# Writing a sampling table in larger pieces, with the image blocks kept in SBUF and two late writes

## The chip, the core and the metric

The kernel runs on one core of one Trainium2 chip. The metric is the device time of one execution in microseconds, the median of three runs. Profiles are taken in an execution of their own, in which every instruction is recorded; that one ran longer (8957 us) than the timed ones (7859 us). Times of single instructions below are from that profile.

## The reference

Four layers run one after the other on an input of 4 images, 256 channels, 64 x 64 pixels, all in float32. Each layer normalises its input (group norm, 32 groups), applies a block and adds the input. Only the first block matters here, a deformable convolution:

```
y    = leaky_relu(bn(conv1x1(gn(x))))                       # 256 -> 256
xp   = y @ inproj_w.T + inproj_b                            # values to be sampled
t    = leaky_relu(bn(depthwise3x3(y)))
offset, mask = t @ off_w.T + off_b, softmax(t @ mask_w.T + mask_b)
samp = bilinear sample of the padded xp, 4 groups of 64 channels,
       9 points a pixel and group, at place + 6 * tap + offset
dout = sum over the 9 points of samp * mask, then outproj
x2   = bn(y + dout); squeeze-and-excite; fc1, leaky_relu, fc2; result y + mlp
```

The three others are a linear attention block with depthwise 5x5 convolutions, a 3x3 convolution with binarised weights, and an attention block over pooled keys.

## The kernel before

An image is held as 128 partitions (channels) by two halves of channels (`KT` = 2) by 4096 pixels, and worked on in eight blocks of 512 pixels, which is eight rows of 64.

**Sampling.** For each image n the values xp lie in device memory in a table `tab[n]` of shape [4 groups, 66, 67, 2, 64]: at a place (y, x) it has the 64 channels of a group for this row (s = 0) and for the row below (s = 1). So 1024 bytes in a row are all four neighbours that a bilinear sample needs, and every value stands in the table twice. `sample(n)` goes over the points in rounds of 14 pixels. A round issues four gathers on GpSimd (L592, 128 places each, one a group), TensorE sums them with the weights that VectorE made (`wm`, L583), and later steps transpose, project and add. There are 1172 gathers an image. The gathered data have seven buffers of four.

**What makes the table.** `convolve(n)` first loads the image's eight blocks for the statistics (L334), computes the group norm, and writes zeros to the table's edges (L347 to L353, 48 small writes). Then `steps()` (L405) goes over the blocks again, in half blocks of 128 output channels: it loads x once more (L409; tag `x`, four buffers); `convolved` makes the 1x1 convolution in PSUM (L367), whose leaky relu gives `yc` (L369 on ScalarE, L370 on VectorE); `spread` copies it into the padded tiles of the depthwise convolution and writes the block to `y_d[n]` (L376); `projected` multiplies `yc` by `inproj_w` with pixels on the output's partitions (L387): 128 pixels at a time, thus two rows of the image; `added` adds the bias into `xo` (L391) and makes x + y + bias in place in x (L393), which goes to `xy_d[n]` (L396) for the end of the layer. Last come 16 writes of a block's `xo` to the table (L401), of 256 pieces of 256 bytes each:

```
for r in range(2):          # which of the two rows of a tile of 128 pixels
    for s in range(2):      # as this row, or as the row below
        for j in range(4):  # which tile
```

`offsets` works on chunks of two blocks: depthwise 3x3 (L185, L187), offsets and mask (L486 to L489), coordinates and weights (`coordinates`), which go to `s_d[n]` (L542). `sample` reads them back as `sl` (L572, L573).

**Order of the work.** `run` interleaves generators by shares of their cost (`beside`). In the start-up `convolve(0)` and the first chunk of `offsets` run alone, and every engine's order is made by the framework's scheduler from priorities (the order of the program text) and its cost model. Afterwards sections with `ordered()` keep the order of the program text on TensorE, VectorE, ScalarE and GpSimd; the DMA queue of SyncE (SP) is ordered by the scheduler throughout, and executes in that order. Five such sections matter: `sample(0)` beside `convolve(1)` to `convolve(3)` and the remaining offsets; `sample(1)` beside the binarising of weights, the feed-forward and linear attention of image 0; `sample(2)` and `sample(3)` beside the later layers of the images before; and then a tail without sampling.

Of the kernel before, what the change touches and what calls it, by code (L numbers as in the profile page):

```python
# [9 lines left out]
F32 = mybir.dt.float32  # L10
I32 = mybir.dt.int32
AF = mybir.ActivationFunctionType
ALU = mybir.AluOpType
# [4 lines left out]
P = 128  # L18
N, C, H, W = 4, 256, 64, 64
HW = H * W  # L20
KT = C // P
NB = HW // 512
NT = HW // P
G, PT = 4, 9
# [46 lines left out]

class Net:
    def __init__(self, ctx, tc, a, out):
        self.tc, self.nc, self.a, self.out = tc, tc.nc, a, out
        e = ctx.enter_context
        self.cp = e(tc.tile_pool(name="const", bufs=1, side="left"))
        self.ps1 = e(tc.tile_pool(name="ps1", bufs=1, space=PSUM))
        self.mm = e(tc.tile_pool(name="mm", bufs=3, space=PSUM))
        self.banks, self.alone = cycle(["mm"]), False
        self.dp = e(tc.tile_pool(name="scratch", bufs=1, space=DRAM))  # L80
# [246 lines left out]
    def convolve(self, n, w, sp, bp, pads, used):  # L327


        nc, a = self.nc, self.a  # L330
        src = a["x"][n].rearrange("(k p) s -> p k s", p=P)
        st = sp.tile([P, KT, NB, 6], F32, name="st")
        for b in range(NB):
            self.stats(st, self.block(bp, src, b, "x", bufs=4), b)  # L334
            yield 1.5
        sc, bi = yield from self.groupnorm(sp, st, "g0")
        cw = sp.tile([P, KT, C], F32, name="cwf")
        sh = self.folded(sp, cw, w["cw"], sc, bi, "g0")
        nc.vector.tensor_tensor(sh, sh, self.sh[:, 0:KT], ALU.add)
        low = sp.tile([P, KT], F32, name="low")  # L340
        nc.vector.tensor_scalar(low, sh, SLOPE, None, ALU.mult)
        yield 4


        tab, z = self.tab[n], self.zero
        for g in range(G):
            nc.sync.dma_start(tab[g, 0, :, 0, :], z[0:TX, 0:64])  # L347
            nc.sync.dma_start(tab[g, TY - 2, :, 1, :], z[0:TX, 0:64])
            nc.sync.dma_start(tab[g, TY - 1].rearrange("x s c -> x (s c)"), z[0:TX, 0:P])
            for xx in (0, TX - 2, TX - 1):  # L350
                nc.sync.dma_start(tab[g, 1:TY - 2, xx].rearrange("y s c -> y (s c)"), z[0:TY - 3, 0:P])
                nc.sync.dma_start(tab[g, 0, xx:xx + 1, 1, :], z[0:1, 0:64])
                nc.sync.dma_start(tab[g, TY - 2, xx:xx + 1, 0, :], z[0:1, 0:64])  # L353
        yield 2

        new = lambda c: self.padded(bp, KT, 18, 1, c, bufs=3)
        rw = lambda v: v.rearrange("p (r w) -> p r w", w=W)

        later, now = {}, 0

        def after(lag, f, *args):
            later.setdefault(now + lag, []).append(partial(f, *args))

        def convolved(b, x, yb, m):
            ps = self.ps1.tile([P, 512], F32, name="cv", tag="vk")
            for k in range(KT):
                nc.tensor.matmul(ps, cw[:, k, m * P:(m + 1) * P], x[:, k], start=k == 0, stop=k == KT - 1)  # L367
            t = bp.tile([P, 512], F32, name="lk")
            after(1, lambda: nc.scalar.activation(t, ps, AF.Identity, bias=low[:, m:m + 1], scale=SLOPE))  # L369
            after(1, lambda: nc.vector.scalar_tensor_tensor(yb[:, m], ps, sh[:, m:m + 1], t, ALU.add, ALU.max))  # L370
            after(2, spread, b, yb, m)

        def spread(b, yb, m):
            self.spread({c: p[:, m] for c, p in own.items()}, rw(yb[:, m]), b, 1)
            if m:
                nc.sync.dma_start(self.y_d[n][:, :, b * 512:(b + 1) * 512], yb)  # L376
                c, h = divmod(b, 2)
                for ready in [c - 1] * (b > 0 and not h) + [c] * (b == NB - 1):
                    pads.append((n, ready, own.pop(ready)))

        def projected(b, x, yb, xo, j2):

            ps = self.ps().rearrange("p (j o) -> p j o", o=C)
            for j in range(2):
                at = (2 * j2 + j) * P
                for k in range(KT):
                    nc.tensor.matmul(ps[:, j], yb[:, k, at:at + P], w["iw"][:, k], start=k == 0, stop=k == KT - 1)  # L387
            after(1, added, b, x, yb, xo, j2, ps)

        def added(b, x, yb, xo, j2, ps):  # L390
            nc.vector.tensor_tensor(xo[:, 2 * j2:2 * j2 + 2, :], ps,  # L391
                                    self.row("inproj_b").unsqueeze(1).to_broadcast([P, 2, C]), ALU.add)
            nc.vector.scalar_tensor_tensor(x[:, j2], yb[:, j2], self.vec("fc2_b", j2), x[:, j2], ALU.add, ALU.add)  # L393
            if not j2:
                return
            nc.sync.dma_start(self.xy_d[n][:, :, b * 512:(b + 1) * 512], x)  # L396
            for r in range(2):
                for s in range(2):
                    for j in range(4):
                        yi = 8 * b + 2 * j + r + 1 - s  # L400
                        nc.sync.dma_start(  # L401
                            tab[:, yi, 1:W + 1, s, :].rearrange("g x c -> x g c"),
                            xo[r * 64:(r + 1) * 64, j, :].rearrange("p (g c) -> p g c", g=G))

        def steps():  # L405
            last = None
            for b in range(NB + 1):
                if b < NB:
                    x = self.block(bp, src, b, "x", bufs=4)  # L409
                    yb = bp.tile([P, KT, 512], F32, name="yc", bufs=3)  # L410
                for m in range(KT):
                    if b < NB:
                        if not m and (not b or b % 2 and b // 2 + 1 < NCH):
                            need[now + 1] = (b + 1) // 2
                        convolved(b, x, yb, m)
                    yield 2
                    if last:
                        if not m:
                            xo = bp.tile([P, 4, C], F32, name="xo")
                        projected(*last, xo, m)  # L420
                    yield 2
                last = b, x, yb

        own, need = {}, {}
        for cost in steps():
            yield cost
            now += 1
            if now in need:
                while len(own) + len(pads) - len(used) > 2:
                    yield 0  # L430
                own[need[now]] = new(need[now])
            for f in later.pop(now, ()):
                f()
# [869 lines left out]
```

## Time and profile before

| What | Value |
|---|---|
| Time, median of 3 | 7858.98 us (7857.48 to 7888.82) |
| Span of the profiled execution | 8957.1 us |
| Busy share PE, DVE, ACT, POOL | 67%, 58%, 24%, 58% |
| First gather of images 0, 1, 2, 3 at | 189.8, 1983.3, 3751.3, 5591.8 us |
| Last gather of image 3 at | 7429.4 us |
| DMA moved | 1059 MB, 819976 packets, 464320 of them under 512 bytes |
| Table writes (L401) | 512, 64 KB each |
| Loads of the input x | 64, 512 KB each |

PE is the matrix engine (PEld its loading of weights), DVE the vector engine, ACT the scalar engine, POOL GpSimd, SP the engine that issues DMAs. A group of instructions is shown by line, engine, operation, and what it writes and reads; then the busy time in us, the mean of one in ns, and the idle time of the engine in front of it, with what ended most of that. A float32 matrix product appears in the records as two passes.

### The profile page before, as it was taken

How to read it: one execution, taken by the hardware profiler on the slowest of the kernel's cores; microseconds unless marked ns; L12 is line 12 of the kernel's file. 1: busy time of each engine (PE TensorE's matmuls, PEld its weight loads, DVE VectorE, ACT ScalarE, POOL GpSimd, SP SyncE). 2: the span in 40 equal slices, each digit the busy share in tenths (PEclk: the TensorE clock that was granted, in tenths of full speed). 3: DMA queues.
4: the chain of work that ended last, by engine and by line, in shares of the span. 5: the costliest groups of instructions: out<-in, count | busy, mean ns of one | idle time of the engine just before them, and what ended most of it. 6: DMA issues, size and time to landing. Idle time of an engine off the chain costs nothing. (4 is left out here: it accounts for less than half of the span.)

```text
span 8957.1 us, 94935 instructions
## 1 busy us (share of the span) xinstructions
PE 6029.8 (67%) x36020; PEld 3636.8 (41%) x36020; DVE 5176.0 (58%) x6393; ACT 2190.6 (24%) x4899; POOL 5162.6 (58%) x4950
## 2 busy tenths in 40 slices
PE   3354554447744447688776677887766778987899
PEld 2232332223422223244554443345544433664477
DVE  4344443443366667524777776227777772599734
ACT  1111111112211111122223222222232222455424
POOL 1666666566666666666666656666666561376410
PEclk7566675668866667799987787898878889998899
DMA  6455454445533334444443334444544333220131
GB/s 166 119 152 158 135 160 130 131 125 161 161 105 104 104 106 124 122 133 135 133 138 110 110 112 135 139 136 128 142 116 115 108 116 97 71 71 27 45 96 55
DMA packets 819976, 1059.01 MB, mean 118 GB/s; under 512 B 464320, under 2 KB 524864, under 8 KB 817984
## 3 DMA queue, kind: packets, MB, share of 16 engines
q0 software_dynamic: 225024, 614.77, 23.9%
q1 hardware_dynamic: 594496, 438.18, 17.1%
q8 instruction: 285, 4.67, 0.2%
q14 instruction: 171, 1.40, 0.0%
HBM read 883.86 MB, written 168.69 MB: 118 GB/s over the span
## 5 line engine op out<-in xcount | busy, mean ns | idle before, releaser
L592 POOL DMA_INDIRECT g<-tab,sl x4688 | 4628.4, 987 | 2800.6 <-issue 1224.9
L185 DVE SCALAR_TENSOR_TENSOR agg<-pad,vec,agg 128x1024 f32<-128x1024 f32 x2280 | 2934.3, 1287 | 61.7
L599 PE MATMUL acc<-g,wm 128*32 128x128 f32 x18752 | 1027.0, 336 | 2144.7 <-ACT at L604 1593.1
L599 PEld LDWEIGHTS acc<-g,wm 128*32 128x32 f32 x18752 | 564.6, 129 | 2620.9 <-ACT at L604 1791.9
L583 DVE TENSOR_TENSOR wm<-con,sl 128x1024 f32<-128x1024 f32 (+1 forms) x296 | 358.2, 1211 | 720.7 <-remote 575.2
L1018 PE MATMUL ps<-xd,w 128*128 128x256 f32 x3072 | 746.0, 395 | 31.5 <-issue 23.6
L624 ACT COPY dT<-dp 64x112 f32<-64x112 f32 x1176 | 286.9, 244 | 1543.1 <-remote 734.7
L1018 PEld LDWEIGHTS ps<-xd,w 128*128 128x128 f32 x3072 | 594.8, 199 | 150.7 <-issue 66.9
L717 PE MATMUL ps<-x2f,f 128*128 128x512 f32 x1024 | 503.1, 642 | 7.1 <-ACT f L708 4.0
L788 PE MATMUL ps<-xr,qw 128*128 128x512 f32 x768 | 474.4, 750 | 21.4 <-issue 8.2
L174 DVE SCALAR_TENSOR_TENSOR hm<-ps,vec,lk 128x512 f32<-128x512 f32 x256 | 190.7, 750 | 497.5 <-ACT lk L173 394.4
L724 PE MATMUL ps<-hm,f 128*128 128x512 f32 x1024 | 457.7, 601 | 0.1
L604 ACT COPY at<-acc 128x256 f32<-128x256 f32 (+1 forms) x588 | 218.5, 372 | 731.3 <-remote 670.3
L969 POOL TENSOR_TENSOR xd<-xp 128x640 f32<-128x640 f32 x64 | 79.5, 1270 | 507.0 <-ACT xp L981 412.7
L632 PE MATMUL po<-dT,ow 128*128 128x224 f32 (+1 forms) x1216 | 318.2, 414 | 51.5 <-DVE hm L174 15.6
L836 ACT COPY kt<-pt 128x512 f32<-128x512 f32 x256 | 149.7, 585 | 792.1 <-remote 350.7
L173 ACT ACTIVATE lk<-ps,low 128x512 f32<-128x512 f32 x256 | 174.1, 687 | 625.2 <-PE ps L717 479.1
L1128 PEld LDWEIGHTS ps<-gt,pT 128*128 128x128 f32 x2048 | 288.9, 222 | 70.7 <-issue 40.4
L1128 PE MATMUL ps<-gt,pT 128*128 128x128 f32 x2048 | 302.1, 309 | 17.3 <-ACT pT L1124 11.7
L201 POOL TENSOR_TENSOR ak<-ak,m 128x1024 f32<-128x1024 f32 x96 | 227.9, 2373 | 147.1 <-ACT m L200 143.6
L1108 PE MATMUL s<-ph,th 128*128 128x512 f32 x512 | 289.3, 674 | 26.8 <-ACT kt L836 10.0
L632 PEld LDWEIGHTS po<-dT,ow 128*128 128x128 f32 x1216 | 263.3, 231 | 105.7 <-issue 46.4
(243 smaller groups left out, 8071.3 us busy)
## 6 DMA issues: line engine op xcount, KB each, us to landing
g<-tab,sl POOLq DMA_INDIRECT x4688
x<-x SPq DMA_DIRECT2D x128, 512.0 KB
xr<-x SPq DMA_DIRECT2D x96, 512.0 KB
x<-in_x SPq DMA_DIRECT2D x64, 512.0 KB
tab<-xo SPq DMA_DIRECT2D x512, 64.0 KB
y<-yc SPq DMA_DIRECT2D x32, 512.0 KB
x2f<-x SPq DMA_DIRECT2D x32, 512.0 KB
xyf<-x SPq DMA_DIRECT2D x32, 512.0 KB
```

Source lines behind the costliest of these rows:

```text
L185: nc.vector.scalar_tensor_tensor(to, s, wt, acc, ALU.mult, ALU.add)
L583: nc.vector.tensor_tensor(wm[:, 0:nu], self.con("own").unsqueeze(1).unsqueeze(1).to_broadcast(sh), sl[:, r:r + nu, G:].unsqueeze(3).to_bro ...
L592: nc.gpsimd.indirect_dma_start(out=g[:, i, :], out_offset=None, in_=table, in_offset=bass.IndirectOffsetOnAxis(ap=sl.bitcast(I32)[:, r, i: ...
L599: nc.tensor.matmul(acc[32 * i:32 * i + 32, :], wm[:, r4, 4 * i + 2 * x:4 * i + 2 * x + 2, :], g[:, i, x * P:(x + 1) * P], start=x == 0, st ...
L624: nc.scalar.copy(dT[b][hs, :, q0:q0 + m * (v1 - v0)].rearrange("p g (v o) -> p g v o", o=m), dp[u][hs, v0:v1, :, s, 0:m].rearrange("p v g ...
L632: nc.tensor.matmul(po[m][:, 0:np_], self.ow[:, k, m * P:(m + 1) * P], dT[b][:, k, 0:np_], start=k == 0, stop=k == G - 1)
L717: nc.tensor.matmul(ps, f1[:, k, m * P:(m + 1) * P], x2[:, k], start=k == 0, stop=k == KT - 1)
L724: nc.tensor.matmul(ps, f2[:, k, m * P:(m + 1) * P], hm[:, k], start=k == 0, stop=k == 4 * KT - 1)
L788: nc.tensor.matmul(ps, qw[:, k, m * P:(m + 1) * P], x[:, k], start=k == 0, stop=k == KT - 1)
L1018: nc.tensor.matmul(ps[:, e], w[:, k, t, 2 * half + e, m * P:(m + 1) * P], v[:, 2 * half + e, k, t:t + 8], start=i % 6 == 0, stop=i % 6 == 5)
L1108: nc.tensor.matmul(s[i], tv[:, 4 * b + j], ph[:, i * 512:(i + 1) * 512], start=True, stop=True)
L1128: nc.tensor.matmul(ps[:, 0:P], pT[:, m], gt[:, m], start=m == 0, stop=m == 7)
```

## The change

The change has four parts, all in `convolve`:

1. **Pieces of 512 bytes.** The projection is made so that partitions 0 to 63 hold the pixels of one image row out of the block's upper four, and partitions 64 to 127 those of one out of the lower four. `xo` becomes [128, group, 4 rows, 64]. Two rows that follow each other now lie beside each other in one partition, as s = 0 and s = 1 of a place in the table, so three writes of 256 pieces of 512 bytes for each half, and two with pieces of 256 bytes for the first and last row, take the place of eight: ten a block instead of sixteen. The bytes are the same.
2. **A matching projection.** 64 pixels a product instead of 128: twice as many products, each into one half of the partitions.
3. **Blocks kept.** The eight blocks loaded for the statistics stay in SBUF (eight buffers instead of four) and are used again.
4. **Late writes.** For image 0 the writes of y and of the sum xy are put off in the program text until `convolve(1)` begins. In the other images xy is written after the table's writes.

```diff
+        for to, v in self.kept:
+            nc.sync.dma_start(to, v)
+        xs, self.kept = [], []
         for b in range(NB):
-            self.stats(st, self.block(bp, src, b, "x", bufs=4), b)
+            xs.append(self.block(bp, src, b, "x", bufs=NB))
+            self.stats(st, xs[b], b)
...
+        def write(to, v):
+            if n:
+                nc.sync.dma_start(to, v)
+            else:
+                self.kept.append((to, v))
...
-                nc.sync.dma_start(self.y_d[n][:, :, b * 512:(b + 1) * 512], yb)
+                write(self.y_d[n][:, :, b * 512:(b + 1) * 512], yb)
...
-            for j in range(2):
-                at = (2 * j2 + j) * P
-                for k in range(KT):
-                    nc.tensor.matmul(ps[:, j], yb[:, k, at:at + P], w["iw"][:, k], ...)
+            for r in range(2):
+                for h in range(2):
+                    at = (4 * h + 2 * j2 + r) * W
+                    for k in range(KT):
+                        nc.tensor.matmul(ps[64 * h:64 * h + 64, r], yb[:, k, at:at + W], w["iw"][:, k], ...)
...
-            nc.sync.dma_start(self.xy_d[n][:, :, b * 512:(b + 1) * 512], x)
-            for r in range(2):
-                for s in range(2):
-                    for j in range(4):
-                        yi = 8 * b + 2 * j + r + 1 - s
-                        nc.sync.dma_start(
-                            tab[:, yi, 1:W + 1, s, :].rearrange("g x c -> x g c"),
-                            xo[r * 64:(r + 1) * 64, j, :].rearrange("p (g c) -> p g c", g=G))
+            for h in range(2):
+                v = xo[64 * h:64 * h + 64]
+                y = 8 * b + 4 * h
+                for r in range(3):
+                    nc.sync.dma_start(tab[:, y + r + 1, 1:W + 1].rearrange("g x s c -> x g (s c)"),
+                                      v[:, :, r:r + 2].rearrange("p g r c -> p g (r c)"))
+                nc.sync.dma_start(tab[:, y + 4, 1:W + 1, 0, :].rearrange("g x c -> x g c"), v[:, :, 3])
+                nc.sync.dma_start(tab[:, y, 1:W + 1, 1, :].rearrange("g x c -> x g c"), v[:, :, 0])
+            write(self.xy_d[n][:, :, b * 512:(b + 1) * 512], x)
...
-                    x = self.block(bp, src, b, "x", bufs=4)
+                    x = xs[b]
...
-                            xo = bp.tile([P, 4, C], F32, name="xo")
+                            xo = bp.tile([P, G, 4, 64], F32, name="xo")
```

More of the change, by code (lines that the diff above doesn't have):

```diff
@@ L73, in __init__ @@
     def __init__(self, ctx, tc, a, out):
-        self.tc, self.nc, self.a, self.out = tc, tc.nc, a, out
+        self.tc, self.nc, self.a, self.out, self.kept = tc, tc.nc, a, out, []
         e = ctx.enter_context
@@ L381, in projected @@
         def projected(b, x, yb, xo, j2):
-            ps = self.ps().rearrange("p (j o) -> p j o", o=C)
-            for j in range(2):
-                at = (2 * j2 + j) * P
-                for k in range(KT):
-                    nc.tensor.matmul(ps[:, j], yb[:, k, at:at + P], w["iw"][:, k], start=k == 0, stop=k == KT - 1)
+            ps = self.ps().rearrange("p (r o) -> p r o", o=C)
+            for r in range(2):
+                for h in range(2):
+                    at = (4 * h + 2 * j2 + r) * W
+                    for k in range(KT):
+                        nc.tensor.matmul(ps[64 * h:64 * h + 64, r], yb[:, k, at:at + W], w["iw"][:, k], start=k == 0, stop=k == KT - 1)
             after(1, added, b, x, yb, xo, j2, ps)
         def added(b, x, yb, xo, j2, ps):
-            nc.vector.tensor_tensor(xo[:, 2 * j2:2 * j2 + 2, :], ps,
-                                    self.row("inproj_b").unsqueeze(1).to_broadcast([P, 2, C]), ALU.add)
+            gc = lambda v: v.rearrange("p r (g c) -> p r g c", g=G)
+            nc.vector.tensor_tensor(xo[:, :, 2 * j2:2 * j2 + 2].rearrange("p g r c -> p r g c"), gc(ps),
+                                    gc(self.row("inproj_b").unsqueeze(1).to_broadcast([P, 2, C])), ALU.add)
             nc.vector.scalar_tensor_tensor(x[:, j2], yb[:, j2], self.vec("fc2_b", j2), x[:, j2], ALU.add, ALU.add)
```

## The prediction, as it was put on record before the result

> **What bounds the kernel now.** I read the page first, then busy time by stretch, then the waits and the timeline of the first stretch. From the page (busy time; the slices of two rows; two groups and three lines of the DMA issues):
>
> ```profile
> PE 6029.8 (67%) x36020; PEld 3636.8 (41%) x36020; DVE 5176.0 (58%) x6393; ACT 2190.6 (24%) x4899; POOL 5162.6 (58%) x4950
> ...
> POOL 1666666566666666666666656666666561376410
> PEclk7566675668866667799987787898878889998899
> ...
> L592 POOL DMA_INDIRECT g<-tab,sl x4688 | 4628.4, 987 | 2800.6 <-issue 1224.9
> ...
> x<-in_x SPq DMA_DIRECT2D x64, 512.0 KB
> tab<-xo SPq DMA_DIRECT2D x512, 64.0 KB
> y<-yc SPq DMA_DIRECT2D x32, 512.0 KB
> ```
>
> No engine is full. POOL is evenly loaded from slice 2 to slice 33: those are the four gathering stages, 1172 gathers each. Slice 1 has none: the kernel first makes table 0. Busy time by stretch (start-up, the four gathering stages, the tail), cut at the first gather of each image:
>
> ```profile
> 46.00:190.00 144.00, 78.72 (x224) 44.28 (x222) 70.46 (x99) 26.33 (x48) 0.24 (x1) 0.78 0.64 148
> 190.00:1983.00 1793.00, 801.26 (x6260) 504.58 (x6261) 789.10 (x1041) 248.22 (x689) 1164.22 (x1172) 0.65 0.51 141
> 1983.00:3751.00 1768.00, 1046.22 (x6812) 554.16 (x6812) 1051.96 (x1052) 341.62 (x869) 1161.09 (x1172) 0.74 0.42 122
> 3751.00:5591.00 1840.00, 1372.30 (x8667) 818.62 (x8665) 1147.99 (x1368) 456.50 (x1108) 1152.58 (x1172) 0.85 0.44 127
> ```
>
> Columns are length, then PE, PEld, DVE, ACT, POOL busy, clock, DMA share, GB/s. The reader is to see that a gathering stage lasts about 1800 us whatever stands beside it: the stage with the changed convolution has the least PE and DVE work and 1793 us, one with 571 us more PE work has 1840. The changed work of images 1 to 3 lies beside gathers; that of image 0 lies in front of them, in the first 190 us. There, the waits of the first 190 us, and the timeline of one block of image 0 (start, length, engine, line):
>
> ```profile
> POOL g L592 <- DMA sl<-sd: 188.4, 1, 188.4
> ...
> PE cv L367 <- DMA x<-in_x: 32.9, 5, 15.9
> ```
>
> ```profile
> 113.76 2.87 SPq L401 DMA_DIRECT2D tab<-xo  x4
> ...
> 116.68 0.61 SPq L154 DMA_DIRECT2D x<-in_x  x1
> 117.39 0.54 SPq L396 DMA_DIRECT2D x<-x  x1
> 118.02 8.75 SPq L401 DMA_DIRECT2D tab<-xo  x12
> ...
> 121.41 3.78 PE L367 MATMUL cv<-x,cwf 128*128 128x512 f32 x4 [5.35 <-DMA x<-in_x]
> ```
>
> SP issues table writes from 60 to 185 us, one each 0.66 us (128 starts in the trace), and the reload of x stands among them. So PE waits for x, at half clock, then SP waits for yc (5.4 us at 107.8, 3.6 at 126.8, 5.9 at 144.2, 3.0 at 165.3), and so on: the two queue up behind each other. The last table write and the sl load behind it release the first gather at 189.8.
>
> **What the Trainium skill says.** "DMA: Bandwidth & Descriptors", Specifications: writes under 512 bytes are below line rate and read before they write. The trace agrees in direction: a 256-byte packet took 24.6 ns during the start-up, a 512-byte packet 27.7 (the zero edges of the table). The same page, Anatomy of one DMA: a wait for a semaphore is held on the issuing sequencer, so all behind it stand still; the four SP waits above show it. "TensorEngine Tiling (Array Packing)", Key Properties: column tiles work independently, changing the tiling mode drains the array. The trace has a 128*64 matmul (L871): the passes of one half follow each other at 0.43 us; where the other half's are queued, both run at once (starts at 3388.457 and 3388.463). "TensorE: Matmul & The Clock Gate", Part 1: an idle PE falls to half clock. It shows: four cv passes took 1.98 us in dense work, 3.78 after a wait.
>
> **The change part by part.**
>
> 1. x is kept. 32 loads of 512 KB go. For image 0, the four of them at 41.7 us stood behind 48 zero writes, so convolution began at 45.5; its other operands were ready at 30.2 (L341 ends then). Gain at the front 15 us. Then PE no longer waits for x behind table writes: the rest of the 33 us, and what follows from it on SP, is freed.
>
> 2. Table writes: 10 instead of 16 a block. Each still has 256 pieces (64 pixels by 4 groups), so I keep 0.66 us an issue: 80 x 0.66 = 53 us for image 0 instead of 84. By packets: 12288 x 27.7 ns + 8192 x 24.6 ns over 16 engines = 34 us instead of 50. If a 512-byte write costs SP 1.3 us, which I don't expect (the pieces are as many), it is 48 x 1.3 + 32 x 0.66 = 84 again. I take 53.
>
> 3. y and xy of image 0 are written after its convolution's program text. SP is not ordered by hand, so they become late in rank, not necessarily in time: yc has 3 buffers, so five y writes must still go out in between. 16 x 0.6 = 10 us of SP and 8.4 MB. Their cost is nothing if they fall in SP's gaps; if all come at the first gather, image 1's x loads wait on their landing (buffers are full), and DVE with them: at the 150 GB/s of this stretch 56 us for all, 7 for the first two. Behind a waiting statistics instruction on DVE stands the weighting (L583), and behind it PE's product of the gathers; data there is 27 us ahead (median from landing to PE). I take 0 and keep 20 as an upper end.
>
> 4. The projection has rows in halves: 16 passes of 256 columns a half block instead of 8. In the dense part of the start-up 8 took 1.89 us. Serial: 3.8; if the halves overlap wholly: 1.9. They alternate after 4 passes, so I take 2.8: +0.9 each, 16 in the start-up, 48 beside the gathers (+45 us there, serial at half clock +3.4 each, 163).
>
> 5. The order of additions, the strided output of L391 and xy after the table writes: the same number of DVE instructions, 0.69 us each, taken at the same.
>
> The start-up after, from 30.2: PE has cv 16 x 1.98 = 31.7, projection 16 x 2.8 = 45, offsets 3.3 (32 passes), 2 for the cold start: 82 (67 to 97). DVE: 48 of 0.73 = 35, depthwise of chunk 0 18 x 1.29 + 4 more of 1.28 = 28, its coordinates 12: 75. SP: 53 + 10 from about 44.5 when the first xo is there, to 108. So PE is last: 30 + 82 + about 10 for gaps between the three = 122; then 0.7 for the last sum, some 5 for the last writes, and 4.5 from the sl issue to the first gather (185.3 to 189.8): 132. Gain 189.8 - 132 = 58 us, with the PE ends 43 to 73. The profiled execution took 8957 us where the plain one takes 7859; scaled by 0.877 it is 51 to 58. I take 53.
>
> Beside gathers: +45 us of PE in 1793 where it is busy 801; 24 x loads and 144 table writes fewer. In the windows of 100 us of this stage PE was busy 24 us with 69 gathers and 60 us with 69 gathers; in the next stage 89 us with 65. Gathers near bursts of table writes had an excess over 1.26 us of 0.24 us each, those away from them 0.24 too (the two gaps over 10 us aside). So neither pays: 0. The two gaps of 24 and 19 us near 1660 and 1767 come at runs of offset work on DVE, unchanged. Sum: 7859 - 53 = 7806.
>
> **The rivals.**
>
> A. The start-up stays long: PE serial at half clock (16 x 6.8 = 109 for the projection alone), or the late writes of y and x stop SP. For: PE ran at 0.78 clock there. Against: its idle goes with the x waits. Gain 15 to 25: about 7840.
>
> B. Extra PE work is on the path of the first gathering stage, since PE takes gathers 27 us after they land, so it and not POOL sets the pace at times. 120 of the 163 us serial, less 53, and the 20 of part 3: 7859 + 120 x 0.877 - 53 + 20 = about 7930, slower. Against: the windows above.
>
> C. Smaller DMA load speeds the gathers as well: POOL's wait marked remote is 211 us here and 102 in the third stage; if the excess of 109 goes, 7806 - 96 = 7710. Against: the second stage has 181 without table writes, and bursts show no effect.
>
> **How the numbers follow.** Forecast 0.6, A 0.2, B 0.1, C 0.1. The forecast's spread is the PE ends, 43 to 73 scaled and 20 for late writes: 7790 to 7840, most of it under 7820 (0.5% is 39 us). The range 7760 to 7865 holds nearly all of it, A and the near parts of C: 8 in 10. Faster: 0.6 x 0.85 + C, with a little of A: 0.63. Within: the rest of the forecast, most of A, a little of B: 0.27. Slower: B: 0.10.
>
> **What would show it.** First gather near 132 us in the profile; no PE wait on x in L367; 320 table writes at about 0.66 us; x from the input loaded 32 times; a projection line of 1024 passes with under twice the busy time; the first gathering stage within 20 us of 1793; later stages as before. Wrong if the first gather comes after 165, if an issue with 512-byte pieces takes over 1 us, or if the first stage changes by over 40 us.

## The result, and the profile after

| | Before | After |
|---|---|---|
| Time, median of 6 | 7874.28 us (7857.48 to 7888.82) | 7813.84 us (7807.37 to 7824.31) |
| Ratio | | 0.9927, 95% interval 0.9911 to 0.9944 |
| First gather of image 0 | 189.8 us | 138.2 us |
| Start of the first convolution (L367, now L378) | 45.5 us | 28.8 us |

The gain is 0.73% (0.56% to 0.89%), 57 us of 7874; 53 were forecast.

From the page of the changed kernel: busy time, the packets, the group of gathers, two groups of DMA issues.

```profile
PE 6076.6 (78%) x36532; PEld 3569.4 (46%) x36532; DVE 5166.6 (66%) x6393; ACT 2192.3 (28%) x4899; POOL 5130.7 (66%) x4950
...
DMA packets 759050, 1042.27 MB, mean 133 GB/s; under 512 B 362432, under 2 KB 472128, under 8 KB 757056
...
L607 POOL DMA_INDIRECT g<-tab,sl x4688 | 4596.8, 981 | 1699.8 <-issue 1307.4
...
tab<-xo SPq DMA_DIRECT2D x192, 128.0 KB
x<-in_x SPq DMA_DIRECT2D x32, 512.0 KB
```

Under 512 bytes there are 101888 packets fewer. POOL's idle time in front of the gathers, 2800.6 before and 1699.8 here, must not be booked to the change: that profile of before is of an execution of 8957 us, this one of 7821, and such a difference of pace also stood between two sets of runs of one and the same kernel (8817 and 7819 us for the changed one), so spans are compared only inside one set below. It isn't the recording that made the first profile long: this one is of one of the six timed executions. A gather itself took 987 ns on average there and 981 here; the difference lies in the waits between the gathers. For the same reason PE's busy time (6029.8 before) is better compared in set 1 below: there it rose by 17 us with the change, although it has 512 passes more, and PEld's fell by 34 (6036.7 and 3626.6 in before_again, 6053.4 and 3592.9 in direct_writes).

Busy time by stretch of the changed kernel, the start-up and the first gathering stage (length, then PE, PEld, DVE, ACT, POOL, clock, DMA share, GB/s):

```profile
28.00:138.00 110.00, 75.26 (x357) 37.91 (x357) 70.28 (x101) 26.24 (x48) 0.00 (x0) 0.85 0.62 138
138.00:1661.00 1523.00, 992.70 (x6726) 526.96 (x6726) 798.65 (x1059) 249.06 (x692) 1157.60 (x1172) 0.70 0.56 160
```

The start-up has the same DVE work as before (70 us) in 110 us in place of 144 from the first convolution on. Now what it waits for: the longest waits of the first 200 us of the changed kernel.

```profile
POOL g L607 <- DMA sl<-sd: 136.9, 1, 136.9
...
PE cv L378 <- DVE yc L381: 19.4, 3, 17.1
```

No wait of PE for x is left (32.9 us before). A single new one of 17.1 us has come, for `yc`. The timelines of the changed kernel around it, PE, DVE and then SP (start, length, engine, line; a length over several instructions has their gaps in it):

```profile
57.99 3.67 PE L399 MATMUL ps<-iw,yc 128*64 128x256 f32 x28
78.79 3.78 PE L378 MATMUL cv<-x,cwf 128*128 128x512 f32 x4 [17.12 <-DVE yc L381]
```

```profile
67.24 10.56 DVE L185 SCALAR_TENSOR_TENSOR agg<-pad,vec,agg 128x1024 f32<-128x1024 f32 x8
77.91 0.28 DVE L464 MEMSET pad<- 128x36 f32 x3
78.10 0.63 DVE L381 SCALAR_TENSOR_TENSOR yc<-cv,g_add,lk 128x512 f32<-128x512 f32 x1
```

```profile
69.39 0.63 SPq L417 DMA_DIRECT2D tab<-xo  x1
70.07 1.29 SPq L334 DMA_DIRECT2D y<-yc  x2
71.40 0.87 SPq L334 DMA_DIRECT2D x<-x  x1
...
126.11 3.03 SPq L414 DMA_DIRECT2D tab<-xo  x3
129.18 0.69 SPq L416 DMA_DIRECT2D tab<-xo  x1
...
133.31 0.62 SPq L417 DMA_DIRECT2D tab<-xo  x1
133.97 0.60 SPq L587 DMA_DIRECT2D sl<-sd  x1
```

The late writes (L334) were put in rank behind the 30 table writes of three blocks. Until the first `y<-yc` at 70.1 has gone out and landed, none of the three buffers of `yc` is free. By the trace's semaphore records it had landed at 73.2. DVE then still had the taps of a depthwise convolution in its order (L185, without a pause from 67.2 to 77.8); it writes the fourth block's first `yc` at 78.1, and PE starts again at 78.8. So up to 73.2 the buffer held PE, and some 5 of the 17 us are DVE's order, which the scheduler made. At the end, the last ten table writes all stand behind the last sum `xo` (125.5 to 126.2): 8 us of SP, when PE has been done since 122.6. Between PE's end and that sum DVE had work of `offsets` in its order.

The projection's own instructions, of before and after (count, lowest, median and highest ns, first and last start):

```profile
L387 PEld LDWEIGHTS ps<-iw,yc x512: 186/191/338, 53.5 to 1931.0; 128*128 128x128 f32 x171
L387 PE MATMUL ps<-iw,yc x512: 376/380/796, 54.1 to 1931.3; 128*128 128x256 f32 x171
```

```profile
L399 PEld LDWEIGHTS ps<-iw,yc x1024: 132/137/232, 37.9 to 1599.5; 128*64 128x64 f32 x171
L399 PE MATMUL ps<-iw,yc x1024: 379/379/689, 37.9 to 1599.9; 128*64 128x256 f32 x171
```

One pass lasts as long as before, and there are twice as many. Yet the timeline has 16 of them in 1.95 to 2.00 us (eight took 1.89): the two halves run at the same time, and the trace has their passes start in pairs, 7 ns apart.

### The profile page after: what moved, and what is told of

Its sections match the earlier page's. It is cut to its first block, busy times and chain, and to the rows that moved or that the text cites. A ratio compares the mean times of both kernels' runs of the same rounds, so it can differ in the third digit from the quotient of the medians.

```text
span 7820.6 us, 95715 instructions
## 1 busy us (share of the span) xinstructions
PE 6076.6 (78%) x36532; PEld 3569.4 (46%) x36532; DVE 5166.6 (66%) x6393; ACT 2192.3 (28%) x4899; POOL 5130.7 (66%) x4950
## 5 line engine op out<-in xcount | busy, mean ns | idle before, releaser
L607 POOL DMA_INDIRECT g<-tab,sl x4688 | 4596.8, 981 | 1699.8 <-issue 1307.4
L185 DVE SCALAR_TENSOR_TENSOR agg<-pad,vec,agg 128x1024 f32<-128x1024 f32 x2280 | 2933.8, 1287 | 61.8
L614 PE MATMUL acc<-g,wm 128*32 128x128 f32 x18752 | 1305.8, 319 | 1191.1 <-ACT at L619 625.8
L614 PEld LDWEIGHTS acc<-g,wm 128*32 128x32 f32 x18752 | 639.5, 120 | 1888.0 <-ACT at L619 862.5
L1033 PE MATMUL ps<-xd,w 128*128 128x256 f32 x3072 | 713.1, 385 | 7.4 <-DVE x L1013 3.2
L1033 PEld LDWEIGHTS ps<-xd,w 128*128 128x128 f32 x3072 | 577.7, 193 | 110.3 <-issue 31.6
L732 PE MATMUL ps<-x2f,f 128*128 128x512 f32 x1024 | 476.0, 614 | 4.0 <-ACT f L723 4.0
L803 PE MATMUL ps<-xr,qw 128*128 128x512 f32 x768 | 455.1, 724 | 12.5 <-DVE ot L901 6.4
L740 DVE TENSOR_TENSOR xyf<-xyf,ps 128x512 f32<-128x512 f32 x64 | 44.0, 687 | 421.8 <-PE ps L739 421.8
L647 PE MATMUL po<-dT,ow 128*128 128x224 f32 (+1 forms) x1216 | 287.9, 386 | 30.0 <-DVE yb L651 11.0
L732 PEld LDWEIGHTS ps<-x2f,f 128*128 128x128 f32 x1024 | 191.8, 194 | 232.0 <-issue 221.1
```

Of the source, the lines that this page charges most:

```text
L185: nc.vector.scalar_tensor_tensor(to, s, wt, acc, ALU.mult, ALU.add)
L607: nc.gpsimd.indirect_dma_start(out=g[:, i, :], out_offset=None, in_=table, in_offset=bass.IndirectOffsetOnAxis(ap=sl.bitcast(I32)[:, r, i: ...
L614: nc.tensor.matmul(acc[32 * i:32 * i + 32, :], wm[:, r4, 4 * i + 2 * x:4 * i + 2 * x + 2, :], g[:, i, x * P:(x + 1) * P], start=x == 0, st ...
L647: nc.tensor.matmul(po[m][:, 0:np_], self.ow[:, k, m * P:(m + 1) * P], dT[b][:, k, 0:np_], start=k == 0, stop=k == G - 1)
L732: nc.tensor.matmul(ps, f1[:, k, m * P:(m + 1) * P], x2[:, k], start=k == 0, stop=k == KT - 1)
L803: nc.tensor.matmul(ps, qw[:, k, m * P:(m + 1) * P], x[:, k], start=k == 0, stop=k == KT - 1)
```

## The experiments

Four sets of runs follow, each set beside runs of the kernel before on the same chip. All spans and stage lengths are from one profiled execution of each kernel, cut at the first gather of each image. Ratios are of the times to the kernel before of the set, with 95% intervals.

```
set  kernel          first gather  stages 0 to 3          time      ratio (interval)
1    before_again        185.1     1792 1768 1836 1832   8952.1   0.9996 (0.9988-1.0003)
1    keep_only           156.1     1792 1763 1847 1836   8926.2   0.9966 (0.9954-0.9978)
1    pieces_only         156.8     1796 1762 1833 1829   8907.7   0.9952 (0.9939-0.9965)
1    direct_writes       132.4     1796 1768 1840 1833   8893.1   0.9924 (0.9909-0.9939)
2    after_again         135.3     1769 1750 1825 1808   8825.5   0.9951 (0.9937-0.9966)
2    images_123          166.9     1778 1742 1816 1808   8848.7   0.9969 (0.9959-0.9979)
2    pe_double           134.0     1813 1752 1808 1817   8859.2   0.9987 (0.9980-0.9994)
2    act_half            121.6     1766 1743 1812 1819   8805.8   0.9926 (0.9910-0.9941)
3    after_2             135.3     1521 1516 1558 1573   7813.1   0.9929 (0.9914-0.9943)
3    direct_2            133.2     1521 1510 1557 1569   7808.9   0.9921 (0.9905-0.9938)
3    act_half_late       124.5     1520 1514 1555 1562   7801.2   0.9914 (0.9899-0.9929)
4    act_half_pool       123.2     1522 1516 1561 1573   7818.5   0.9915 (0.9899-0.9930)
```

The kernel before took 8957, 8873, 7872 and 7889 us in the sets 1 to 4.

after_again and after_2 are the changed kernel once more. Of after_again a first gather near 138 us and a ratio of 0.992 to 0.994 were expected; it came out at 135.3 and 0.9951, less of a gain. First gathers of one and the same kernel, profiled twice, differ by 3 us (138.2 and 135.3) and by 5 (189.8 and 185.1), so smaller differences between single profiles show nothing by themselves.

### The parts one by one

**before_again** is the kernel before, unchanged.

> The kernel before, unchanged, for a profile that can be set beside that of the changed one. Theory (all of the gain lies ahead of the first gather): first gather near 190 us, and the four gathering stages, once they are profiled at the pace of the other profile, within 20 us of 1522, 1511, 1554 and 1568. Rival C (the smaller DMA load speeds the gathers): stages of the first image longer than 1522 by 30 us or more.

First gather at 185.1. It took 8952 us like the first profile, not 7821 like the changed kernel's, so its stages stand beside those of its own set only. There they are the same: the four add up to 7228 us here and to 7237 in direct_writes.

**keep_only**, against before:

```diff
-            self.stats(st, self.block(bp, src, b, "x", bufs=4), b)
+            xs.append(self.block(bp, src, b, "x", bufs=NB))
+            self.stats(st, xs[b], b)
...
-                    x = self.block(bp, src, b, "x", bufs=4)
+                    x = xs[b]
```

> Only the blocks of x are kept; sixteen table writes a block, the old projection, no late writes. Theory (SP's issue of writes and PE's waits for x queue up behind each other): convolution starts near 29 us, then SP is last, 128 writes of 0.66 us and 16 others from about 45 us: first gather near 145 to 155 us, the time 35 to 45 us under the kernel before. Rival R1 (the x waits are all of it): the first gather at 138, the whole gain of about 57 us. Rival R2 (the table writes are all of it): only the 15 us at the front, first gather near 175.

First gather 29.0 us earlier, at 156.1, just past the theory's range; the time fell by 0.0034 x 8957 = 30 us (20 to 41), a little under the theory's 35 to 45. SP's timeline in keep_only shows why it stops there:

```profile
74.97 11.38 SPq L403 DMA_DIRECT2D tab<-xo  x16
86.44 0.56 SPq L378 DMA_DIRECT2D y<-yc  x1
87.05 0.62 SPq L398 DMA_DIRECT2D x<-x  x1
87.76 11.37 SPq L403 DMA_DIRECT2D tab<-xo  x16
```

Every write follows the one before it without a pause, 12.8 us a block. With x kept, SP's queue sets the end: PE is done at 118.7, and in the 103 us from 47 to 150 SP's gaps of over 0.1 us add up to 1.1.

**pieces_only** is the changed kernel with x loaded again (the lines above reversed) and y and xy written in place.

> Only the table writes in pieces of 512 bytes with their projection; x is loaded again, no late writes. Theory: convolution starts near 45 us and still waits on x, but behind fewer writes: first gather near 160 to 170 us, the time 20 to 30 us under the kernel before. Rival R1: no gain, within 10 us. Rival R2: first gather near 153 us, gain 35 to 40 us.

First gather 28.3 us earlier, at 156.8; time 0.0048 x 8957 = 43 us less (31 to 55). It is better than the theory's 160 to 170 and 20 to 30, and nearer to rival R2. The theory had left the waits for x in place; but with six writes fewer a block, SP reaches the loads of x sooner, and of the waits of PE for x only the one of 15.9 us at the front and two of 0.33 and 1.20 us are left.

**direct_writes** is both together, without the late writes:

```diff
         def write(to, v):
-            if n:
-                nc.sync.dma_start(to, v)
-            else:
-                self.kept.append((to, v))
+            nc.sync.dma_start(to, v)
```

> The changed kernel with the writes of y and xy of image 0 issued in place. Theory (late writes are worth nothing, 10 us of SP in its gaps): the time within 10 us of the changed kernel, first gather at 138 to 145 us. Rival (the late writes free SP or the transfers for the table): first gather 10 us or more later than 138, time 10 to 20 us above the changed kernel. Rival (late writes stop SP for the buffers of yc, the idle stretch of 17 us of PE near 62 to 79 us in the changed kernel): first gather near 125 us, time 10 to 15 us below the changed kernel.

First gather at 132.4 and ratio 0.9924. The two parts add: 29 + 28 = 57 us separately, 53 together. So neither R1 nor R2 holds; each takes about half. Of this run's own expectations none was met: 132.4 lies between the theory's 138 to 145 and the last rival's 125. Its PE and SP at the end of the start-up:

```profile
105.81 1.95 PE L396 MATMUL ps<-iw,yc 128*64 128x256 f32 x14 [1.30 <-DVE yc L378]
108.75 1.97 PE L396 MATMUL ps<-iw,yc 128*64 128x256 f32 x16 [1.00 <-DVE xo L401]
```

```profile
123.06 1.95 SPq L411 DMA_DIRECT2D tab<-xo  x3
...
125.71 0.62 SPq L414 DMA_DIRECT2D tab<-xo  x1
...
127.05 0.60 SPq L584 DMA_DIRECT2D sl<-sd  x1
```

PE is done at 110.7, without the stop of 17 us, and the last sum at 111.5, but SP at 126.3. SP, not PE, is last.

### The late writes

No set so far has both kernels, so the two ran again in one set.

> The changed kernel once more, so that it and direct_2 share a chip. Theory (late writes of y hold the three buffers of yc, PE stops 17 us near 60 to 77 us, but SP, which sets the end, loses only some 5 us): first gather at 135 to 138 us; ratio to the kernel before 0.992 to 0.996.

> The changed kernel with y and xy of image 0 written in place, as direct_writes. Theory: no stop of 17 us on PE, first gather 3 to 6 us earlier than in after_2, time 0 to 8 us shorter. Rival (late writes pay, by fewer transfers ahead of the first gather): time 5 us or more longer than after_2.

First gather 2.1 us earlier with direct writes, where 3 to 6 were expected; time 4.2 us less, with intervals that overlap. The late writes buy nothing that can be measured. Their stop of PE is real, and mostly hidden: without it PE is done at 110.6 in place of 119.5, but SP's last table write at 126.9 in place of 130.7.

### Only what stands ahead of the first gather?

**images_123** has the changes for images 1 to 3 alone; image 0 has the old projection, sixteen writes a block, and x loaded again (into eight buffers).

> direct_writes for images 1 to 3 alone; image 0 has the old projection, sixteen table writes a block, and loads x again. Theory (only the work ahead of the first gather counts): first gather near 185 to 190 us, the time within 10 us of the kernel before, ratio 0.999 to 1.001. Rival C (fewer loads and writes beside the gathers speed them up): ratio 0.998 or less, with the first gathering stage 20 us shorter than 1791.

The expectation failed: first gather at 166.9 and 27 us less time (0.0031 x 8873; 19 to 36), a ratio that rival C had named. Yet most of this isn't from images 1 to 3. The first gather alone is 18 us earlier than the 185.1 of set 1, because eight buffers let all eight loads go out in one row ahead of the table writes; SP's timeline of images_123:

```profile
41.58 5.04 SPq L154 DMA_DIRECT2D x<-in_x  x8
```

Loading x twice costs 15.9 us at the front (the only wait of PE for x that is left there). The waits that followed in the kernel before came from four buffers and sixteen writes together: with eight buffers they are gone here, and with ten writes they were nearly gone in pieces_only. The other 9 us stay unplaced: set 2 has no profile of the kernel before, and in set 1 no stage became shorter with the change.

A cleaner reading is beside after_again, in the same set: that has the change in image 0 too. Its first gather is 31.6 us earlier and its time 23 us less (8825.49 and 8848.69), while the four stages add up to 7152 us there and to 7144 here. What image 0 adds lies ahead of the first gather.

**pe_double** is the changed kernel with the projection of images 1 to 3 made twice:

```diff
-            for r in range(2):
+            for r in [0, 1] * (2 if n else 1):
```

> The changed kernel with the projection of images 1 to 3 made twice (the second overwrites the first): 48 x 16 more passes, 1.95 us a set of 16, so 94 us more PE work beside the gathers of image 0. Theory (PE work there is hidden): the first gathering stage and the time within 10 us of the changed kernel. Rival B (it lies on the path): 40 to 94 us longer.

Time 32 us more than after_again (0.0036 x 8873), first stage 43 us more: between theory and rival B. PE's busy time in that stage rose by 131 us (821.6 to 952.6), not by 94. POOL's waits in front of the gathers from 190 to 1750 us, after_again and then pe_double (total, times, longest; in "issue" nothing that the profile shows holds the engine, and of "remote" it can't tell what ended the wait):

```profile
POOL g L607 <- issue: 280.0, 916, 0.8
POOL g L607 <- remote: 166.1, 71, 3.8
POOL g L607 <- PE acc L614: 66.9, 14, 23.8
```

```profile
POOL g L607 <- issue: 273.1, 893, 1.1
POOL g L607 <- remote: 147.2, 76, 3.3
POOL g L607 <- PE acc L614: 127.7, 25, 36.4
```

PE frees the buffers of the gathers (L614). With more work it frees them later, 61 us more of waiting. By hundreds of gathers, the growth lies in the tenth and eleventh (169 and 165 us become 182 and 188), where before had its two long gaps. So PE is on the path there, and about a third of the 131 us of extra work comes through to the stage. This holds for set 2. In after_2, whose stage lasts 1521 us, POOL waited for PE at L614 for 9 us in the same stage and not 67; what extra work of PE would cost there was not run.

### Half of the table writes on a second queue

**act_half** is direct_writes with half the table writes of image 0 on the queue of ScalarE:

```diff
             for h in range(2):
+                q = nc.sync if n or not h else nc.scalar
...
-                    nc.sync.dma_start(tab[:, y + r + 1, 1:W + 1]...
+                    q.dma_start(tab[:, y + r + 1, 1:W + 1]...
```

(and the same for the two other writes).

> direct_writes, with the table writes of a block's lower half (partitions 64 to 127) of image 0 issued from the queue of ScalarE. Theory (in the start-up SP's issuing sets the end: 80 table writes and 16 others, 126 us, while PE's last product ends at 110.7): SP has 27 us less, PE and DVE become last: first gather near 115 to 120 us, the time 10 to 16 us under direct_writes. Rival (the transfers or PE set the end): first gather at 128 to 133 us, time within 5 us of direct_writes. Rival (ScalarE's issues delay the leaky relu and with it PE): first gather after 133 us.

First gather at 121.6, a little later than the theory's 115 to 120, and 13.7 us ahead of after_again; time 19.6 us less than it (8805.84 and 8825.49), ratio 0.9926 against 0.9951, with intervals that just overlap. That SP's queue was last is shown. Busy time from the first table writes to the last, direct_writes and then act_half:

```profile
45.00:127.00 82.00, 56.99 (x317) 29.92 (x316) 61.98 (x91) 21.94 (x41) 0.00 (x0) 0.93 0.84 201
```

```profile
45.00:117.00 72.00, 57.66 (x314) 30.44 (x308) 61.19 (x90) 21.87 (x41) 0.00 (x0) 0.96 0.93 259
```

Whether all of it is SP's issuing is not shown, because the packets became cheaper too. Among the table's writes one of 512 bytes took 42.7 ns on average in direct_writes and 34 here, one of 256 bytes 25.4 and 21, although the DMA engines moved more (259 GB/s against 201). With 84% of their time taken before, the transfers alone did not set the end, but they were close behind.

**act_half_late** is the same with the late writes of the changed kernel.

> The changed kernel, late writes and all, with half of the table writes of image 0 issued from the queue of ScalarE. Theory (with SP relieved, the stop of PE for the buffers of yc is on the path): first gather later than the 121.6 us of act_half, at 125 to 132 us, the time between act_half (0.9926) and the changed kernel. Rival (the 17 us stop never matters): first gather at 120 to 122 us.

First gather at 124.5, just short of the forecast 125; time 11.9 us less than after_2, with intervals that overlap. But the stop that the theory was about did not come. The first late write of y went out at 56.8, not at 70.1, and PE's longest wait for `yc` is 1.6 us. PE where the stop stood before:

```profile
62.51 1.99 PE L378 MATMUL cv<-x,cwf 128*128 128x512 f32 x4 [1.23 <-DVE yc L381]
...
67.39 1.98 PE L378 MATMUL cv<-x,cwf 128*128 128x512 f32 x4 [1.48 <-DVE yc L381]
```

So this run doesn't tell what the stop would cost with SP relieved, and its 3 us beside the 121.6 of act_half are no more than two profiles of one kernel differ by.

**act_half_pool** takes the sums x + bias + y of image 0 from VectorE as well:

```diff
+            if n:
                 nc.vector.scalar_tensor_tensor(x[:, j2], yb[:, j2], ...)
+            else:
+                nc.gpsimd.tensor_scalar(x[:, j2], x[:, j2], self.vec("fc2_b", j2), None, ALU.add)
+                nc.gpsimd.tensor_tensor(x[:, j2], x[:, j2], yb[:, j2], ALU.add)
```

> act_half, with the sums x + bias + y of image 0 moved from VectorE (16 of 0.74 us) to GpSimd, which is idle ahead of the first gather, as two operations each (a sum of 128x1024 took GpSimd 2.36 us in the tail of the kernel before, so 1.2 us for half of that: some 40 us in all). Theory (in act_half VectorE is the engine that leaves no gaps from 60 to 110 us): 12 us of VectorE go, first gather at 112 to 118 us, ratio to the kernel before 0.990 to 0.992. Rival (PE, or the issuing on both queues, holds the end): first gather at 120 to 123 us. Rival (GpSimd and VectorE hinder each other): first gather after 123 us.

A miss: 123.2, where 112 to 118 was expected. The ratio lies in the range of 0.990 to 0.992, but is no gain beside act_half_late's 0.9914. The stretch from 60 to 110 us of act_half_pool:

```profile
60.00:110.00 50.00, 44.04 (x244) 23.21 (x241) 41.98 (x62) 17.11 (x31) 30.37 (x21) 1.00 0.93 261
```

DVE has 42.0 us in place of act_half's 47.4, but PE stays at 44 of 50 and the DMA engines at 93%. DVE's lack of gaps didn't mean that it set the end. There is something for the third rival as well: while GpSimd worked, four of DVE's operations for the coordinates took 1.57, 1.70, 0.86 and 0.83 us, in act_half 0.75, 0.71, 0.45 and 0.45, 2.6 us more in all. Whether PE, the transfers or this held the end was not told apart.

## Why the prediction came true, step by step

The mechanism and the sum were right: the gain lies ahead of the first gather, 51.6 us in the profiles against 58 forecast, and 57 of time (44 to 70) against 53. Rival A would have had 15 to 25, B a longer time; rival C fell with the stages of set 1, which are as long with the change (7237 us) as without (7228). No profile of the kernel before was had in an execution of 7870 us, so at that pace the stages were not compared. By its letter one sign of the forecast failed, the first stage within 20 us of 1793: it has 1523 in the first profile of the changed kernel. That is the pace of the execution; in set 1 it is 1796 against 1792.

The step from 58 to 53, the scaling by 0.877, had no ground: the start-up doesn't follow the pace. The changed kernel's first gather is at 135.3 us in an execution of 8817 us and in one of 7819, direct_writes' is at 132.4 and, as direct_2, at 133.2. Inside the sum of 58, several terms were off, and two of them cancelled.

1. **x kept.** Right: convolution starts at 28.8, 16.7 us earlier (15 forecast). keep_only shows it alone to be worth 30 us. What the waits in the middle came from was read only half: they need the four buffers as well as the table writes (images_123, pieces_only), and not only the loads.
2. **Table writes.** An issue took 0.62 us and 0.66 with the gap to the next, with pieces of 512 bytes as of 256. The 53 us were right: SP was busy 62.5 us with 92 issues from 44.6 to 134 us, against 53 + 10. The packet price was wrong: the 27.7 ns for 512 bytes were taken from the zero edges and set beside 24.6 for 256 bytes from the table's writes. On the zero edges 256 bytes took only 17.9 ns, and among the table's writes in after_again 512 bytes took 43.3 on average, so 12288 x 43.3 + 8192 x 25.2 ns over 16 engines is 46 us, not 34. It stayed hidden behind the issuing.
3. **Late writes at no cost.** Their price was right within the measurement (direct_2 4 us faster, intervals overlapping), but not "in SP's gaps": with them PE stops for 17 us, some 5 of which are DVE's order.
4. **Projection.** 2.8 us for 16 passes was mis-sized; it was 1.95, so 16 x 0.85 = 14 us less on PE in the start-up. Beside the gathers of image 0, PE's busy time rose by 39 us in set 1 (800.9 in before_again, 839.8 in direct_writes), near the 45 forecast, and the stage grew by 4. But that such work is free there was too strong: in set 2 pe_double paid 32 us for 131. Had the halves not overlapped, rival B might have been partly right.
5. **Order and strided xo.** Right: 0.68 us an addition.

**PE is last, first gather at 132.** PE's end was forecast at 122 and measured at 122.6, and at 119.5 and 119.6 in after_2 and after_again. That is luck: 14 us too much for the projection stood against the stop of 17 us that was priced at nothing. Without late writes PE ended at 110.7 (110.6 in direct_2), and the first gather came only 2.1 us sooner in the same set. So what is wrong is "PE is last": SP's 63 us of issuing can't run without pause, and its queue needs nearly as long with or without the stop. SP waited 23 us for `xo` and in the stop (11 in direct_writes from the same moment on), and the last block's ten writes take 8 us after the last sum, where "some 5" were put. These 3 us stand in all profiles of the changed kernel. The other 3 between 132 and 138, by which the last addition ended later (126.2, forecast 122.7), do not: in after_2 and after_again it ended at 123.0 and 123.1, and the first gather came at 135.3.

## What to carry to other kernels

Where a serial front feeds a long stage, count the issuing queue like an engine, with its pauses and with the last batch that can only start after the last result; here moving half of the writes to a second engine's queue brought the first gather forward by 11 to 14 us. A write that is put off holds the buffer it reads from: ask what the next writer of that buffer waits for before calling it free. And a price taken in one place (the 512-byte packets of the zero edges, PE work beside gathers that wait for something else) is an estimate in another. It isn't load alone that changes it: with two queues the packets were cheaper while the DMA engines were busier.

## What was not expected of the hardware

Two sets of products with 64 weight columns each, into the two halves of the partitions, overlapped almost wholly: 16 passes in 1.95 to 2.00 us where eight with 128 columns took 1.89, and a weight load took 137 ns in place of 191 in the median. A table write of 256 pieces took SP 0.62 us whether the pieces had 256 or 512 bytes. On ScalarE's queue it was 0.66 us in the median, with 12 of the 40 over 1 us, while the activations between them kept their 0.69 us. A packet of 512 bytes took 43 ns on average among the table's writes and one of 256 bytes 25; on the zero edges they took 27.7 and 17.9. With half of the table's writes on ScalarE's queue they were at 34 and 21, with medians of 27 and 18, the DMA engines being busier (93% against 84%). What makes the difference stays open. GpSimd added a bias to 128x512 floats in 1.57 us and two such tiles in 1.27 us, where VectorE did both in one operation of 0.74.
